# Two transformer layers with self- and cross-attention: rows of maxima and cross queries in four transfers each instead of eight

## The chip, the cores and the metric

The kernel runs on one core of a Trainium2 chip. The metric is the device time of one execution in microseconds, as the median of several runs. The core's engines are TensorE (PE in the profile, its weight loads PEld), VectorE (DVE), ScalarE (ACT), GpSimd (POOL) and SyncE (SP), which here only issues DMA transfers.

## The reference

Two layers work on x of shape (4, 512, 320) in float32. Each layer is self-attention, cross-attention to a context of 1601 positions and 192 channels, and a gated feed-forward block. There are 20 heads of 16 channels.

```
def _attn(x, ctx, wq, wk, wv, wo, bo, heads):     # dh = 16, scale = dh ** -0.5
    sim = einsum('bhid,bhjd->bhij', q, k) * scale
    a = softmax(sim, axis=-1)
    out = einsum('bhij,bhjd->bhid', a, v)
    return out @ wo + bo

h1 = _ln(x, n1_g, n1_b); x = _attn(h1, h1,      q1, k1, v1, o1_w, o1_b, 20) + x
h2 = _ln(x, n2_g, n2_b); x = _attn(h2, context, q2, k2, v2, o2_w, o2_b, 20) + x
h3 = _ln(x, n3_g, n3_b)
a, g = split(h3 @ ff_w1 + ff_b1, 2)
x = a * gelu(g) @ ff_w2 + ff_b2 + x
```

## The kernel before

**Units.** The attention of one batch is cut into five groups of four heads. One such group is a unit, and the kernel works through 20 self units, 20 cross units and 4 feed-forward units per layer, one after the other. A self unit has 512 keys in 4 chunks of 128, a cross unit 1601 keys in 13 chunks, the last of 65.

**Layout.** Each of a unit's four heads has a slot of 32 partitions, so that four products with 32 contraction rows can stand in four row strips of TensorE. Numbers are split in a high part (rounded to the fast float32 format) and a low part. In a slot of `kT` the even rows hold high parts of the keys and the odd rows low ones. Queries are copied to both, in `u.qbuf` of [128, 2, 512]: e = 0 holds the high part and e = 1 the low part, each as 512 columns. A score is then two passes, e = 0 and e = 1, which add up in PSUM.

**Maxima and scores.** For softmax the maximum of each query's scores is needed. Scores are therefore made twice: once with the queries on the partitions (`passes`, L1007), from which VectorE takes maxima (L1026), and once with the keys on the partitions (`product`, L1186), from which ScalarE makes the exponential (L1199). The maxima of the next unit are taken beside the scores of the present one; `round_of` issues scores of two heads and maxima of two others together. Two such rounds go by for each chunk, 8 in a self unit and 26 in a cross unit.

**`max_end` (L1067).** It turns a unit's negated maxima into rows. The high parts are 16 columns (4 heads by 4 query tiles), the low parts 16 more; VectorE transposes the [128, 32] tile in blocks of 32 (L1074), and DMA transfers then take rows of it to `u.mrow`: in the slot of head j the high part goes to row 32j and the low part to row 32j + 1. That is a transfer for each of four blocks and for each of the two parts, eight per unit, 2 KB each (L1080). `less_maximum` (L1189) is a third pass, which adds these two rows to every key's scores: `units_of`, all ones, is its stationary operand, `u.mrow[two_rows]` the moving one. The exponential waits for it. There are two `mrows`, used in turn.

**`queries` (L788).** It projects a unit's queries, ScalarE scales them into a stage tile (L802), `split` makes high and low parts on GpSimd (L695, L696), and transfers (L807) carry them to `u.qbuf`, for two halves i of the 512 columns and for even and odd rows s. A self unit's queries are made in one part, with four transfers of 128 KB. A cross unit's are made in two parts of 128 columns of each half, each with a stage tile and four transfers of 64 KB of its own.

**Order.** The order of all instructions is fixed when the program is built. Small steps stand in queues with due times; one of them, `slots`, holds the transfers that `slots_soon` puts there, of which up to four are given out per round, in order, from two rounds after they were put there. A new stage tile first gives out all older groups but one. A unit's maxima may begin three rounds after its last query and key transfer has been given out (`at_hand`). At the start, transfers are split over SyncE's and ScalarE's queues; from the first unit on all go through SyncE's queue, which takes them strictly in order: a transfer that waits for its data holds up all behind it.

Of the kernel before, what the change touches and what calls it, by code (L numbers as in the profile page):

```python
# [17 lines left out]
B, N, D = 4, 512, 320  # L18
# [108 lines left out]
def kernel(ctx: ExitStack, tc: tile.TileContext, x, context, ws, out):  # L127
# [50 lines left out]

    nmax = [const.tile([P, HG * NQ], F32, name=f"nmax{i}") for i in range(2)]
    kbuf = [const.tile([P, 4 * QT + P], F32, name=f"kT{i}") for i in range(4)]  # L180
    qbuf = [const.tile([P, 2, N], F32, name=f"q{i}") for i in range(4)]

    mrows = [const.tile([P, N], F32, name=f"m{i}") for i in range(2)]
    units_of = const.tile([P, P], F32, name="units")
    nc.gpsimd.memset(units_of, 1.0)
    fill = qbuf[3][:, 0, :]
    see(nc.vector.memset(fill, 1.0))


# [502 lines left out]
    def split(x, high):  # L692

        eng = nc.vector if start["on"] else nc.gpsimd
        eng.tensor_scalar(high.bitcast(F32R), x, 1.0, None, ALU.mult)  # L695
        eng.tensor_tensor(x, x, high, ALU.subtract)  # L696

    def rows_of(t, s):

        return t.rearrange("(r s) n -> s r n", s=2)[s]  # L700
# [10 lines left out]
    def stages(kind="stage"):  # L711
        empty(kind, 1)
        if kind == "kstage":
            kstage.reverse()
            return kstage[0]
        t = two.tile([P, 2, N // 2], F32, tag="stage", name="stage")
        return [t[:, e] for e in range(2)] + [t]

    def slots_soon(us, fs, name, kind="stage"):

        fs = list(fs)
        done = fs.pop()

        def last():
            done()
            for u in us:
                setattr(u, name, -9 if start["on"] else clock["round"])

        group = deque(fs + [last])
        groups[kind].append(group)  # L730
        for u in us:
            u.slots.append(group)
        if start["on"]:
            empty(kind, 0)
        for _ in tuple(group):
            add("slots", 0.0, lambda: group and group.popleft()(), clock["round"] + 3, yes, ready_at(clock["round"] + 2))
# [4 lines left out]
    def add_proj(u):  # L741
# [42 lines left out]
                add(chain, 0.0, hold, due - 4, yes, lambda: "h" in u.own)  # L784

        parts = 2 if u.cross else 1

        def queries(part):  # L788
            w = N // 2 // parts
            at = [i * (N // 2) + part * w for i in range(2)]  # L790
            ps = step_bank([P, 512], "qps")
            for k, _, n in DK:
                for i, to, gs in tiles:
                    see(nc.tensor.matmul(  # L794
                        ps[to, :w],
                        lhsT=wq[:n, k, gs],
                        rhs=first.hT[:n, k, at[i] : at[i] + w],
                        start=(k == 0),
                        stop=(k == 2),
                    ))  # L800
            high, low, both = stages()
            see(nc.scalar.mul(low[:, :w], ps[:, :w], DH**-0.5))  # L802
            split(low[:, :w], high[:, :w])

            def move(s, i):
                queue = (nc.sync, nc.scalar)[s] if start["on"] else nc.sync
                queue.dma_start(  # L807
                    out=u.qbuf.rearrange("(r s) e n -> s r e n", s=2)[s][:, :, at[i] : at[i] + w],
                    in_=both[i * GD : (i + 1) * GD, :, :w],
                )  # L810

            slots_soon(
                [u], [lambda s=s, i=i: move(s, i) for i in range(2) for s in range(2)],
                "qwhen" if part == parts - 1 else "qpart",
            )
            if part == parts - 1:
                u.q = u.qbuf
                first.made["q"] += 1

        def keys():  # L820

# [172 lines left out]
    def max_pairs(u):  # L994

        full = u.nkeys // 512
        rest = u.nkeys - full * 512
        ns = full + (1 if rest else 0)
        u.nm = nmax[u.n % 2]
        u.pm = two.tile([P, NQ, HG, ns], F32, tag="pm", name="pm") if ns > 1 else None  # L1000

        def passes(heads, outs, queries, keys):

            def one_pass(e):
                for j, out in zip(heads, outs):
                    rows = slice(j * SLOT, (j + 1) * SLOT)
                    see(nc.tensor.matmul(  # L1007
                        out,
                        lhsT=u.q[rows, e, queries].bitcast(F32R),
                        rhs=u.kT[rows, keys].bitcast(F32R),  # L1010
                        start=(e == 0),
                        stop=(e == 1),
                    ))

            return [lambda e=e: one_pass(e) for e in range(2)]

        def full_two(heads, t, s):
            pss = [bank("sps") for _ in heads]
            if ns == 1:
                to = u.nm.rearrange("p (j t) -> p j t", t=NQ)[:, :, t]  # L1020
            else:
                to = u.pm[:, t, :, s]

            def reduce():
                for j, ps in zip(heads, pss):
                    see(nc.vector.tensor_reduce(to[:, j : j + 1], ps, AX.X, ALU.max, negate=(ns == 1)))  # L1026

            keys = slice(u.k0 + s * 512, u.k0 + (s + 1) * 512)
            return passes(heads, pss, slice(t * P, (t + 1) * P), keys), reduce

        def rest_two(heads):

            w = rest + rest % 2
            pss = [bank("sps") for _ in heads]
            todo = [
                f
                for t in range(NQ)
                for f in passes(
                    heads, [ps[:, t * w : (t + 1) * w] for ps in pss], slice(t * P, (t + 1) * P),
                    slice(u.nkeys - w, u.nkeys),  # L1040
                )
            ]

            def reduce():
                for j, ps in zip(heads, pss):
                    see(nc.vector.tensor_reduce(
                        u.pm[:, :, j, full], ps[:, : NQ * w].rearrange("p (t w) -> p t w", w=w), AX.X, ALU.max
                    ))

            return todo, reduce  # L1050

        pairs = [
            deque([lambda heads=heads, t=t, s=s: full_two(heads, t, s)] for s in range(full) for t in range(NQ))
            for heads in ((2, 3), (0, 1))
        ]
        if rest:
            for q, heads in zip(pairs, ((2, 3), (0, 1))):
                q.append([lambda heads=heads: rest_two(heads)])
        return pairs
# [7 lines left out]
    def max_end(u):  # L1067

        both = two.tile([P, SLOT], F32, tag="nm2", name="nm2")
        turned = two.tile([P, SLOT], F32, tag="turned", name="turned")  # L1070
        n = HG * NQ
        see(nc.vector.tensor_scalar(both[:, :n].bitcast(F32R), u.nm, 1.0, None, ALU.mult))
        see(nc.vector.tensor_tensor(both[:, n:], u.nm, both[:, :n], ALU.subtract))
        see(nc.vector.transpose(turned, both))  # L1074
        to = u.mrow.rearrange("(j s) (t i r) -> i s j t r", s=SLOT, t=NQ, r=SLOT)
        for i in range(P // SLOT):
            for e in range(2):
                rows = slice(i * SLOT + e * n, i * SLOT + (e + 1) * n)
                queue = (nc.sync, nc.scalar)[e] if start["on"] else nc.sync
                queue.dma_start(out=to[i, e], in_=turned[rows, :])  # L1080

    def add_finish(u):

# [88 lines left out]
    def main(u, give, nxt):  # L1172
# [5 lines left out]
        def score(c, j):  # L1178
            r = min(P, u.nkeys - c * P)
            rows = slice(j * SLOT, (j + 1) * SLOT)  # L1180
            st = bank("st")
            keys = u.kT[rows, u.k0 + u.cols[c] : u.k0 + u.cols[c] + r].bitcast(F32R)
            two_rows = slice(j * SLOT, j * SLOT + 2)

            def product(e):
                see(nc.tensor.matmul(st[:r, :], lhsT=keys, rhs=u.q[rows, e, :].bitcast(F32R), start=(e == 0), stop=False))  # L1186

            def less_maximum():
                see(nc.tensor.matmul(  # L1189
                    st[:r, :],  # L1190
                    lhsT=units_of[two_rows, :r].bitcast(F32R),
                    rhs=u.mrow[two_rows, :].bitcast(F32R),
                    start=False,
                    stop=True,
                ))

            def exponential():
                p = place()
                see(nc.scalar.activation(p[:r], st[:r], AF.Exp))  # L1199
                pr[c, j] = p  # L1200

            return [lambda: product(0), lambda: product(1), less_maximum], exponential
# [357 lines left out]
```

## Time and profile before

| | |
|---|---|
| median of 3 runs | 3174.94 us (3174.68 to 3178.04) |
| profiled execution, its own time | 3173.88 us |
| its span, first to last instruction | 3172.1 us |
| mean granted TensorE clock | 0.971 of full speed |
| busy: TensorE, VectorE, ScalarE, GpSimd | 3005.0, 2193.3, 1965.0, 1269.2 us |

By stages, from the profile's windows (the first product of scores is at 41 us):

| stage | window, us | TensorE busy, us | VectorE busy, us | ScalarE busy, us |
|---|---|---|---|---|
| self, layer 0 | 41 to 427 | 353.49 | 301.43 | 239.51 |
| cross, layer 0 | 427 to 1337 | 860.13 | 725.39 | 701.17 |
| feed-forward, layer 0 | 1337 to 1634 | 295.91 | 81.03 | 43.70 |
| self, layer 1 | 1634 to 2014 | 348.86 | 291.43 | 239.09 |
| cross, layer 1 | 2014 to 2890 | 838.18 | 707.86 | 697.64 |
| feed-forward, layer 1 | 2890 to 3172 | 278.71 | 63.02 | 37.43 |

In the profile's lines, `L1080 SPq` is an issue on SyncE's queue by line 1080 of the kernel; the transfer itself takes place later. `[1.46 <-DMA m<-turned]` behind an instruction says that its engine stood idle for 1.46 us before it, until a transfer into a tile `m` from a tile `turned` had landed.

### The profile page before, as it was taken

To read this page: it belongs to the slowest core of one execution; us is meant where nothing else is said; L and a number is where in the kernel's file an instruction comes from. 1 tells how busy PE (TensorE), PEld (TensorE's weight loads), DVE (VectorE), ACT (ScalarE), POOL (GpSimd) and SP (SyncE) were. 2 spreads that over 40 slices of the span, in tenths; PEclk is the share of its full clock that TensorE was granted. 3 is DMA by queue.
4 is the path that set the end of the run, shared out by engine and by line. 5 is a ranking of instruction groups with operands and counts; after the bars stand their busy time and mean duration, and the time that the engine had idled before them with its cause. 6 is when DMAs were issued, how large, how long until landed. Compare 5 with 4: busy or idle time off the path is not lost.

```text
span 3172.1 us, 94150 instructions
## 1 busy us (share of the span) xinstructions
PE 3005.0 (95%) x37842; PEld 1627.3 (51%) x37842; DVE 2193.3 (69%) x4315; ACT 1965.0 (62%) x4029; POOL 1269.2 (40%) x1449
## 2 busy tenths in 40 slices
PE   8899999999999999999998999999999999999999
PEld 4445455554555455355544555555555555544555
DVE  7778788778778778622256877887888888784221
ACT  3666557777778678811126765587778778785110
POOL 3445334544544444311114453345455455442000
PEclk8999999999999899999999999999999999999999
DMA  4333222211211211300113332222122221112000
GB/s 100 91 71 80 50 43 51 59 38 40 58 37 40 58 33 30 85 2 6 26 25 82 72 64 53 44 54 40 33 47 41 41 48 32 39 23 67 9 11 15
DMA packets 256589, 145.41 MB, mean 46 GB/s; under 512 B 150036, under 2 KB 246680, under 8 KB 256152
## 3 DMA queue, kind: packets, MB, share of 16 engines
q1 hardware_dynamic: 254888, 138.33, 19.8%
q8 instruction: 298, 4.88, 0.6%
q10 hardware_dynamic: 1264, 1.06, 0.2%
q14 instruction: 139, 1.14, 0.1%
HBM read 33.04 MB, written 7.93 MB: 13 GB/s over the span
## 4 chain that ended last, share of the span: by engine, by line
PE 67%; DVE 16%; SPq 5%; DMA 4%; issue 3%; POOL 3%; ACT 2%; ACTq 0%; DVEq 0%; POOLq 0%
PE av L1213 16%; PE st L1186 10%; PE fps L1308 9%; PE sps L1007 9%; DVE pm L1026 8%; PE yps L1363 5%; DVE nmax L1026 3%; PE st L1189 3%; PE ops L1124 3%; PE vps L961 3%; SPq L1080 3%; PE qps L794 2%; PE fps L1321 2%; PE kps L869 2%; DMA kT<-w 1%
## 5 line engine op out<-in xcount | busy, mean ns | idle before, releaser
L1026 DVE TENSOR_REDUCE pm<-sps 128x1 f32<-128x512 f32 x1920 | 1189.6, 679 | 100.8 <-PE sps L1007 89.7
L1007 PE MATMUL sps<-kT,q 32*128 32x512 f32 (+1 forms) x6400 | 1065.4, 408 | 33.3 <-DMA kT<-stage 10.8
L1199 ACT ACTIVATE pr<-st 128x512 f32<-128x512 f32 (+1 forms) x1710 | 906.6, 602 | 252.5 <-PE st L1189 243.6
L1186 PE MATMUL st<-q,kT 32*128 32x512 f32 (+1 forms) x5440 | 947.2, 441 | 32.9 <-ACT w L878 26.3
L1230 POOL TENSOR_TENSOR o<-o,pr 128x512 f32<-128x512 f32 x359 | 461.5, 1286 | 729.3 <-ACT pr L1229 707.3
L1213 PE MATMUL av<-pr,vals 128*32 128x512 f32 (+1 forms) x3420 | 655.0, 627 | 37.1 <-DVE pm L1026 12.1
L1186 PEld LDWEIGHTS st<-q,kT 32*128 32x128 f32 (+1 forms) x5440 | 476.5, 183 | 396.5 <-ACT pr L1199 140.0
L1007 PEld LDWEIGHTS sps<-kT,q 32*128 32x128 f32 x6400 | 552.6, 188 | 136.7 <-DVE pm L1026 25.9
L1189 PE MATMUL st<-m,units 2*128 2x512 f32 (+1 forms) x2720 | 544.9, 401 | 35.1 <-DMA m<-turned 33.2
L1199 ACT ACTIVATE wself<-st 128x512 f32<-128x512 f32 (+1 forms) x867 | 463.6, 602 | 92.6 <-PE st L1189 90.8
L1026 DVE TENSOR_REDUCE nmax<-sps 128x1 f32<-128x512 f32 x640 | 396.3, 679 | 142.1 <-PE sps L1007 110.8
L1213 PE MATMUL av<-wself,vals 128*32 128x512 f32 (+1 forms) x1734 | 380.4, 623 | 12.9 <-DVE pm L1026 7.7
L1230 POOL TENSOR_TENSOR o<-o,wself 128x512 f32<-128x512 f32 x191 | 245.3, 1284 | 329.4 <-ACT wself L1229 326.4
L1189 PEld LDWEIGHTS st<-m,units 2*128 2x128 f32 (+1 forms) x2720 | 254.8, 184 | 71.0 <-issue 39.6
L1331 ACT ACTIVATE pr<-fps,b 128x512 f32<-128x512 f32 x80 | 54.8, 688 | 373.4 <-PE fps L1321 266.1
L1308 PE MATMUL fps<-hT,w 128*128 128x512 f32 x640 | 285.0, 597 | 0.0
L1229 ACT COPY pr<-av 128x512 f32<-128x512 f32 x359 | 218.2, 608 | 35.0 <-PE av L1213 34.0
L1213 PEld LDWEIGHTS av<-pr,vals 128*32 128x32 f32 (+1 forms) x3420 | 91.9, 109 | 208.3 <-DVE pm L1026 98.3
L1308 PEld LDWEIGHTS fps<-hT,w 128*128 128x128 f32 x640 | 118.5, 190 | 149.4 <-issue 147.2
L695 POOL TENSOR_SCALAR stage<-stage 128x256 fp32r<-128x256 f32 (+1 forms) x155 | 107.3, 692 | 184.0 <-ACT stage L802 90.8
L869 PEld LDWEIGHTS kps<-ctxT,w 32*128 32x128 f32 (+1 forms) x4992 | 119.6, 167 | 51.6 <-ACT pr L1199 20.9
L498 POOL TENSOR_SCALAR root<-root 128x4 f32<-128x4 f32 x23 | 5.2, 227 | 326.0 <-DVE root L492 325.5
(100 smaller groups left out, 3297.4 us busy)
## 6 DMA issues: line engine op xcount, KB each, us to landing
kT<-w SPq DMA_DIRECT2D x240, 104.0 KB
q<-stage SPq DMA_DIRECT2D x320, 64.0 KB
q<-stage SPq DMA_DIRECT2D x154, 128.0 KB
aT<-o SPq DMA_DIRECT2D x320, 32.0 KB
m<-turned SPq DMA_DIRECT2D x636, 2.0 KB
kT<-stage SPq DMA_DIRECT2D x156, 64.0 KB
kT<-w SPq DMA_DIRECT2D x80, 72.0 KB
w<-in_L_xattn_ff_w_dram SPq DMA_DIRECT2D x20, 256.0 KB
```

Source lines behind the costliest of these rows:

```text
L695: eng.tensor_scalar(high.bitcast(F32R), x, 1.0, None, ALU.mult)
L869: see(nc.tensor.matmul(ps[to : to + n, :PIECE], lhsT=wk_q[rows, k, u.g * GD : u.g * GD + n], rhs=first.kvT[rows, k, at : at + PIECE], star ...
L1007: see(nc.tensor.matmul(out, lhsT=u.q[rows, e, queries].bitcast(F32R), rhs=u.kT[rows, keys].bitcast(F32R), start=(e == 0), stop=(e == 1),))
L1026: see(nc.vector.tensor_reduce(to[:, j : j + 1], ps, AX.X, ALU.max, negate=(ns == 1)))
L1186: see(nc.tensor.matmul(st[:r, :], lhsT=keys, rhs=u.q[rows, e, :].bitcast(F32R), start=(e == 0), stop=False))
L1189: see(nc.tensor.matmul(st[:r, :], lhsT=units_of[two_rows, :r].bitcast(F32R), rhs=u.mrow[two_rows, :].bitcast(F32R), start=False, stop=True,))
L1199: see(nc.scalar.activation(p[:r], st[:r], AF.Exp))
L1213: see(nc.tensor.matmul(ps[j * SLOT : (j + 1) * SLOT, :], lhsT=columns_of[:r, head : head + SLOT], rhs=pr.pop((c, j))[:r, :], start=True, s ...
L1229: see(nc.scalar.copy(vo, ps))
L1230: nc.gpsimd.tensor_tensor(u.o, u.o, vo, ALU.add)
L1308: see(nc.tensor.matmul(ps, lhsT=w1[:, k, i * FF + c * P : i * FF + (c + 1) * P], rhs=u.hT[:, k, :], start=ahead and k == 0, stop=not ahead ...
L1363: see(nc.tensor.matmul(ps[:, :D], lhsT=hid[c][:, t * P : (t + 1) * P], rhs=w2[:, c, :], start=(c == 0), stop=(c == NHC - 1),))
```

## The change

A unit's maxima go to rows 32j (high) and 32j + 16 (low) of the slot instead of 32j and 32j + 1. The columns of the tile before the transposition are put in the order head, part, tile, so that the 32 rows of one transposed block go out in one transfer to eight rows that lie 16 apart: four transfers of 4 KB per unit. At the start they are two per queue. The other rows of `mrows` are set to zero once, at the start, and `less_maximum` contracts all 32 rows of the slot.

`u.qbuf` becomes [128, 2, 2, 256]: first the half i, then the part e. A half's high and low parts then lie side by side both in the stage tile and in `u.qbuf`. A cross unit's two parts of queries are put into one stage tile, and its four transfers of 128 KB are given out after the second part; each row of a transfer is one piece of 2 KB. `passes` and `product` read the queries from the new places; `product` reads its 512 columns as two pieces of 256.

```
-    qbuf = [const.tile([P, 2, N], F32, name=f"q{i}") for i in range(4)]
+    qbuf = [const.tile([P, 2, 2, N // 2], F32, name=f"q{i}") for i in range(4)]
     mrows = [const.tile([P, N], F32, name=f"m{i}") for i in range(2)]
+    for m in mrows:
+        nc.gpsimd.memset(m, 0.0)
...
         def queries(part):
...
-            high, low, both = stages()
-            see(nc.scalar.mul(low[:, :w], ps[:, :w], DH**-0.5))
-            split(low[:, :w], high[:, :w])
+            if part == 0:
+                made["q"] = stages()
+            high, low, both = made["q"]
+            cols = slice(part * w, (part + 1) * w)
+            see(nc.scalar.mul(low[:, cols], ps[:, :w], DH**-0.5))
+            split(low[:, cols], high[:, cols])
+            if part < parts - 1:
+                return
             def move(s, i):
                 queue = (nc.sync, nc.scalar)[s] if start["on"] else nc.sync
                 queue.dma_start(
-                    out=u.qbuf.rearrange("(r s) e n -> s r e n", s=2)[s][:, :, at[i] : at[i] + w],
-                    in_=both[i * GD : (i + 1) * GD, :, :w],
+                    out=rows_of(u.qbuf[:, i].rearrange("p e n -> p (e n)"), s),
+                    in_=both[i * GD : (i + 1) * GD].rearrange("p e n -> p (e n)"),
                 )
...
-                        lhsT=u.q[rows, e, queries].bitcast(F32R),
+                        lhsT=u.q[rows, t // 2, e, t % 2 * P : (t % 2 + 1) * P].bitcast(F32R),
...
     def max_end(u):
-        n = HG * NQ
-        see(nc.vector.tensor_scalar(both[:, :n].bitcast(F32R), u.nm, 1.0, None, ALU.mult))
-        see(nc.vector.tensor_tensor(both[:, n:], u.nm, both[:, :n], ALU.subtract))
+        high, low = (both.rearrange("p (j e t) -> p e j t", j=HG, e=2)[:, e] for e in range(2))
+        nm = u.nm.rearrange("p (j t) -> p j t", t=NQ)
+        see(nc.vector.tensor_scalar(high.bitcast(F32R), nm, 1.0, None, ALU.mult))
+        see(nc.vector.tensor_tensor(low, nm, high, ALU.subtract))
         see(nc.vector.transpose(turned, both))
-        to = u.mrow.rearrange("(j s) (t i r) -> i s j t r", s=SLOT, t=NQ, r=SLOT)
+        to = u.mrow.rearrange("(n s) (t i r) -> s i n t r", s=DH, t=NQ, r=SLOT)[0]
         for i in range(P // SLOT):
-            for e in range(2):
-                rows = slice(i * SLOT + e * n, i * SLOT + (e + 1) * n)
-                queue = (nc.sync, nc.scalar)[e] if start["on"] else nc.sync
-                queue.dma_start(out=to[i, e], in_=turned[rows, :])
+            queue = (nc.sync, nc.scalar)[i % 2] if start["on"] else nc.sync
+            queue.dma_start(out=to[i], in_=turned[i * SLOT : (i + 1) * SLOT, :])
...
-                see(nc.tensor.matmul(st[:r, :], lhsT=keys, rhs=u.q[rows, e, :].bitcast(F32R), start=(e == 0), stop=False))
+                see(nc.tensor.matmul(st[:r, :], lhsT=keys, rhs=u.q[rows, :, e].bitcast(F32R), start=(e == 0), stop=False))
             def less_maximum():
-                    lhsT=units_of[two_rows, :r].bitcast(F32R),
-                    rhs=u.mrow[two_rows, :].bitcast(F32R),
+                    lhsT=units_of[rows, :r].bitcast(F32R),
+                    rhs=u.mrow[rows, :].bitcast(F32R),
```

More of the change, by code (lines that the diff above doesn't have):

```diff
@@ L180 @@
     kbuf = [const.tile([P, 4 * QT + P], F32, name=f"kT{i}") for i in range(4)]
-    qbuf = [const.tile([P, 2, N], F32, name=f"q{i}") for i in range(4)]
+    qbuf = [const.tile([P, 2, 2, N // 2], F32, name=f"q{i}") for i in range(4)]
     mrows = [const.tile([P, N], F32, name=f"m{i}") for i in range(2)]
+    for m in mrows:
+        nc.gpsimd.memset(m, 0.0)
     units_of = const.tile([P, P], F32, name="units")
     nc.gpsimd.memset(units_of, 1.0)
-    fill = qbuf[3][:, 0, :]
+    fill = qbuf[3][:, 0].rearrange("p e n -> p (e n)")
     see(nc.vector.memset(fill, 1.0))
@@ L786, in add_proj @@
         parts = 2 if u.cross else 1
+        made = {}
         def queries(part):
@@ L807, in move @@
                 queue.dma_start(
-                    out=u.qbuf.rearrange("(r s) e n -> s r e n", s=2)[s][:, :, at[i] : at[i] + w],
-                    in_=both[i * GD : (i + 1) * GD, :, :w],
-                )
[L812 to L818, printed above, removed]
+                    out=rows_of(u.qbuf[:, i].rearrange("p e n -> p (e n)"), s),
+                    in_=both[i * GD : (i + 1) * GD].rearrange("p e n -> p (e n)"),
+                )
+            slots_soon([u], [lambda s=s, i=i: move(s, i) for i in range(2) for s in range(2)], "qwhen")
+            u.q = u.qbuf
+            first.made["q"] += 1
         def keys():
@@ L1000, in max_pairs, with passes @@
         u.pm = two.tile([P, NQ, HG, ns], F32, tag="pm", name="pm") if ns > 1 else None
-        def passes(heads, outs, queries, keys):
+        def passes(heads, outs, t, keys):
             def one_pass(e):
@@ L1028, in full_two @@
             keys = slice(u.k0 + s * 512, u.k0 + (s + 1) * 512)
-            return passes(heads, pss, slice(t * P, (t + 1) * P), keys), reduce
+            return passes(heads, pss, t, keys), reduce
         def rest_two(heads):
@@ L1038, in rest_two @@
                 for f in passes(
-                    heads, [ps[:, t * w : (t + 1) * w] for ps in pss], slice(t * P, (t + 1) * P),
-                    slice(u.nkeys - w, u.nkeys),
+                    heads, [ps[:, t * w : (t + 1) * w] for ps in pss], t, slice(u.nkeys - w, u.nkeys),
                 )
@@ L1182, in score @@
             keys = u.kT[rows, u.k0 + u.cols[c] : u.k0 + u.cols[c] + r].bitcast(F32R)
-            two_rows = slice(j * SLOT, j * SLOT + 2)
             def product(e):
-                see(nc.tensor.matmul(st[:r, :], lhsT=keys, rhs=u.q[rows, e, :].bitcast(F32R), start=(e == 0), stop=False))
+                see(nc.tensor.matmul(st[:r, :], lhsT=keys, rhs=u.q[rows, :, e].bitcast(F32R), start=(e == 0), stop=False))
             def less_maximum():
```

## The prediction

> **What bounds the kernel now.** I read the profile's page first (busy shares and the chain that ended last), then the list of waits, then the timeline round single waits, at last the lines by form for prices. The page:
>
> ```profile
> span 3172.1 us, 94150 instructions
> PE 3005.0 (95%) x37842; PEld 1627.3 (51%) x37842; DVE 2193.3 (69%) x4315; ACT 1965.0 (62%) x4029; POOL 1269.2 (40%) x1449
> PE 67%; DVE 16%; SPq 5%; DMA 4%; issue 3%; POOL 3%; ACT 2%; ACTq 0%; DVEq 0%; POOLq 0%
> ```
>
> TensorE is the bound: busy for 95% of the span, so all the time that any change can win without removing matmuls lies in its 167 us of idle time. The chain's 9% on SyncE's queue and on transfers says that part of that idle time comes from moving data. The list of waits says which part (microseconds in total, times, longest):
>
> ```profile
> PE st L1189 <- DMA m<-turned: 33.2, 25, 6.9
> PE st L1186 <- ACT w L878: 26.3, 15, 2.6
> PE av L1213 <- DVE pm L1026: 19.8, 26, 1.4
> PE av L1213 <- DVE nmax L1026: 13.5, 28, 1.0
> PE sps L1007 <- DMA kT<-stage: 10.8, 5, 2.8
> ```
>
> The largest single wait of TensorE is the one that the change touches: the subtracting product (L1189) waits for the row of maxima, 33.2 us in 25 places. What such a wait consists of shows the timeline of one, in a self unit:
>
> ```profile
> 1904.52 3.35 SPq L1080 DMA_DIRECT2D m<-turned  x6
> 1907.97 2.45 SPq L839 DMA_DIRECT2D kT<-stage  x4
> 1909.12 0.50 PE L1189 MATMUL st<-m,units 2*128 2x512 f32 x2 [1.46 <-DMA m<-turned]
> 1909.68 2.06 ACT L1199 ACTIVATE pr<-st 128x512 f32<-128x512 f32 x4 [1.82 <-PE st L1189]
> 1910.08 1.29 DVE L1026 TENSOR_REDUCE nmax<-sps 128x1 f32<-128x512 f32 x2 [1.22 <-PE st L1189]
> ```
>
> The transfers leave SyncE's queue one after the other; the last is issued by 1907.87 and the product starts 1.25 us later, so the landing is short and the issuing is the long part. In this wait TensorE (1.46), ScalarE (1.82) and VectorE (1.22) all sat idle: no other work was waiting to take its place.
>
> **The change part by part.** *Maxima in four transfers.* One batch of eight, and what an issue costs by its kind:
>
> ```profile
> 105.16 4.64 SPq L1080 DMA_DIRECT2D m<-turned  x8
> ...
> 116.90 2.45 SPq L839 DMA_DIRECT2D kT<-stage  x4
> ...
> L1080 SPq DMA_DIRECT2D m<-turned x636: 520/521/1123, 36.2 to 2860.5; - x159
> L807 SPq DMA_DIRECT2D q<-stage x474: 590/607/1931, 17.6 to 2814.2; - x158
> ```
>
> Eight take 4.64 us, 0.58 each with the step between. An issue of 16 rows (m) takes 521 ns, one of 64 rows (q) 607 ns, so 32 rows should lie between, near the first: four take 2.3 us, and the last maximum is under way 2.3 us earlier. If each doubled in price nothing would be won, if it stayed exactly at 521 ns 2.32; I take 2.3. The landing could grow, as each transfer now holds 4 KB; the 1.25 us above are mostly latency, so I take no change (0.3 more would cost 25 x 0.3 = 7.5 us at most).
>
> Capping each of the 25 waits at 2.3 us leaves only the longest above the cap: 33.2 - (6.9 - 2.3) = 28.6 us.
>
> A cross unit shows the same with a queue in front:
>
> ```profile
> 845.69 2.54 SPq L807 DMA_DIRECT2D q<-stage  x4
> 846.79 0.21 DVE L1074 STREAM_TRANSPOSE turned<-nm 128x32 f32<-128x32 f32 x1
> 848.35 4.62 SPq L1080 DMA_DIRECT2D m<-turned  x8
> 850.05 3.81 DVE L1026 TENSOR_REDUCE pm<-sps 128x1 f32<-128x512 f32 x6 [0.69 <-PE sps L1007]
> 854.12 0.50 PE L1189 MATMUL st<-m,units 2*128 2x512 f32 x2 [1.50 <-DMA m<-turned]
> ```
>
> The maxima were ready at 847.0 but left from 848.35, behind four transfers of half the queries. Here VectorE worked until 853.86, only 0.26 us before the product: what TensorE wins here, it partly meets again as a bank that VectorE has not read.
>
> *What else hangs on the queue.* The eight issues at 105.16 stand ahead of keys in an unbroken row of issues, and TensorE waits for both a query stage and a key:
>
> ```profile
> 104.89 1.51 PE L826 MATMUL kps<-hT,wself 112*32 112x256 f32 x12 [4.87 <-ACT stage L802]
> 120.91 0.49 PE L1007 MATMUL sps<-kT,q 32*128 32x512 f32 x2 [1.68 <-DMA kT<-stage]
> L802 ACT ACTIVATE stage<-qps 128x256 f32<-128x256 f32 x40 | 15.4, 385 | 51.4 <-PE qps L794 36.7 <-DMA q<-stage 7.1 <-DMA aT<-o 2.1
> ```
>
> Of the 10.8 us on keys about 9.8 go when capped at 2.3 each (none is over 2.8), and of the 4.87 us, behind a query transfer (7.1 on ScalarE's side), 2.3.
>
> *The start.* There both queues issue four; now two each:
>
> ```profile
> 36.48 3.24 ACTq L1080 DMA_DIRECT2D m<-turned  x4
> 4.96 0.21 POOL L185 MEMSET units<- 128x128 f32 x1
> 13.72 3.54 POOL L570 TENSOR_TENSOR x<-x,brow 128x320 f32<-128x320 f32 x4 [8.56 <-DMA brow<-in_L_xattn_o_b_dram]
> ```
>
> Two of 0.6 us go: 1.2 us. The two added memsets of 512 columns stand beside the 128-column one of 0.21 us: at most 0.84 us each by columns, inside GpSimd's 8.56 us of idle time before 13.72. Without that cover they would cost 1.7 us.
>
> *Cross queries.* 40 units issue four fewer each: 160 x 0.61 = 98 us less on SyncE's queue, but TensorE meets it only where queries stand ahead of maxima, and there the cap of 2.3 already exceeds the wait of 1.50. What it adds: the first half's transfers now wait for GpSimd's split of the second half, and whatever is queued behind them on SyncE (maxima, keys, attention outputs) waits too. They were needed together before, too (a unit's maxima begin three rounds after the last query transfer is given out), so I price it at nothing; if a round's delay of 1.7 us (876 us of the second cross stage below over 20 units of 26 rounds) hit all 40 units it would cost 68 us. The 26.3 us on L878 stay: they wait for transfers of context keys, whose issue waits for GpSimd's split of them, not for maxima.
>
> *Products.* The subtracting product contracts 32 rows instead of 2, and the main product reads its queries as two pieces of 256:
>
> ```profile
> L1189 PE MATMUL st<-m,units x2720: 384/394/791, 41.1 to 2890.1; 2*128 2x512 f32 x183, 2*65 2x512 f32 x12
> L1186 PE MATMUL st<-q,kT x5440: 382/397/791, 37.4 to 2889.8; 32*128 32x512 f32 x183, 32*65 32x512 f32 x12
> L878 ACT COPY w<-kps 128x104 f32<-128x104 f32 x160 | 31.6, 249 | 100.1 <-PE kps L869 53.9 <-DMA kT<-w 42.2 <-issue 2.2
> L834 ACT COPY stage<-kps 128x256 f32<-128x256 f32 x40 | 14.9, 373 | 48.1 <-PE kps L826 44.4 <-DMA m<-turned 3.2 <-DMA q<-stage 0.6
> L969 ACT COPY vals<-vps 128x192 f32<-128x192 f32 x48 | 13.0, 323 | 32.5 <-PE vps L961 32.5
> ```
>
> Medians of 394 ns for 2 rows and 397 for 32: 3 ns x 2720, two at a time, is 4 us at the very worst and nothing by the minima (384 and 382). For the split read no matmul of this trace is a pattern. The nearest row is ScalarE's: two whole copies (249 ns at 104 columns, 373 at 256) give 0.82 ns a column and 321 ns at 192; the copy that writes its 192 columns in 12 pieces takes 323. A piece costs it nothing, so I take nothing here. The upper end is a second start of a matmul:
>
> ```profile
> L794 PE MATMUL qps<-hT,w 112*32 112x128 f32 x1280 | 51.6, 280 | 0.4 <-DVE pm L1026 0.4
> L794 PE MATMUL qps<-hT,wself 112*32 112x256 f32 x640 | 48.4, 425 | 0.0
> ```
>
> Half the columns save 145 ns, so 135 ns do not depend on them: 5440 passes, two at a time, 2720 x 0.135 = 367 us if it showed in full. Fewer than 512 columns are not streamed, so it can't be a gain.
>
> *The sum.* 28.6 + 9.8 + 2.3 + 1.2 = 42 us of idle time can go. How much comes back: in the self unit 1.22 of 1.46 us were idle on all three engines, in the cross unit only 0.26 of 1.50 on VectorE. Between these (84% and 17%), weighted to the self stages, to which all of the key terms and the longest waits belong, I keep 70%: 29 us. The profiled execution took 3173.88 us, its span and 1.8 us around it; it comes to 3144.9. The median of the three runs lies 1.06 higher, so I predict 3146 us.
>
> [...]
>
> **The rivals.** *The waits are handed on.* After each stall VectorE's reduces (the waits on L1026 above, 19.8 + 13.5 us) or the next transfer end last; kept is the cross unit's share, 17 to 20%: 8 us, 3167. For it: the 3.81 us of reduces before 854. Against: the idle ScalarE and VectorE at 1909.
>
> *Slower by the order.* Fewer query transfers shift the order that the queue of small steps is drained in, so from the first cross stage on the instructions stand in another order than before; the self stages keep theirs. The cross stages hold this much idle time:
>
> ```profile
> 427.00:1337.00 910.00, 860.13 (x12406) 471.36 (x12404) 725.39 (x1397) 701.17 (x1454) 434.76 (x441) 0.97 0.21 47
> 2014.00:2890.00 876.00, 838.18 (x12396) 462.51 (x12393) 707.86 (x1355) 697.64 (x1451) 434.90 (x441) 0.98 0.20 45
> ```
>
> 50 + 38 = 88 us. If worse placed context keys and maxima add half of it, 44, the sum is 15 us slower: 3190. It decides from a third (29 us) on. For it: the waits on L878 and L1026 stand there and hang on such placing. Against: work and rounds are the same, and the queue has less to carry.
>
> *Slower by the split read.* 10 ns for each of 2720 pairs of passes eats the gain; 20 ns give 54 - 29 = 25 us more: 3200.
>
> *It doesn't shorten the wait.* If an issue of 32 rows costs twice one of 16, or landing grows by 2 us, only the start is left: 3173. Against: 607 ns for 64 rows.
>
> **How the numbers follow.** Forecast 0.67 (3146, its own range 3133 to 3163), handed on 0.15, order 0.08, split read 0.06, no shorter wait 0.04. A difference of 0.2% is 6.3 us, about what a measurement of this kernel can tell from none: faster below 3168.6, slower above 3181.3. Faster: 0.67 and half of the second, 0.75; the same: the other half and the last, 0.11; slower 0.14. Range 3125 (all 42 us kept, and 8 won by the order) to 3176 (the last case, and 3 lost by the order): it takes in all but the slower cases.
>
> **What would show it.** Right: four issues of m in 2.3 us; the wait of L1189 for m under 10 us, that of L1007 for keys under 3; span of the self stages down by some 10 us each, that of the cross stages by 4 or 5 each; L1186 still at a median of 397. Wrong: m's issues over 0.8 us each; L1186 longer; idle time before L1213 and L1186 up by as much as m's fell; cross stages longer than 910 and 876 us.

## The result, and the profile after

| | before | after |
|---|---|---|
| median, timed side by side (4 runs each) | 3176.32 us (3174.68 to 3178.04) | 3101.56 us (3099.82 to 3104.63) |
| profiled execution, its own time | 3173.88 us | 3100.62 us |
| mean granted TensorE clock | 0.971 | 0.986 |

The ratio is 0.9766 (95% interval 0.9749 to 0.9783): 75 us faster, where 29 were forecast. The time lies below the predicted range. The changed kernel's page, the first lines and the chain:

```profile
span 3098.8 us, 93413 instructions
PE 2966.7 (96%) x37842; PEld 1615.6 (52%) x37842; DVE 2192.6 (71%) x4315; ACT 1963.5 (63%) x4029; POOL 1269.3 (41%) x1451
PE 70%; DVE 20%; DMA 2%; issue 2%; POOL 2%; ACT 2%; SPq 1%; ACTq 0%; POOLq 0%; DVEq 0%
```

SyncE's queue and transfers fell from 9% of the chain to 3%. The span is 73.3 us shorter, and only half of that is idle time of TensorE: 167.1 us before (3172.1 - 3005.0), 132.1 now (3098.8 - 2966.7), so 35.0. The other 38.3 us are TensorE's *busy* time, 3005.0 to 2966.7, with the same 37842 matmuls. The matmuls themselves became faster.

The list of TensorE's waits (total, times, longest):

```profile
PE st L1187 <- ACT w L882: 27.3, 15, 2.9
PE av L1214 <- DVE pm L1030: 20.5, 28, 1.3
PE av L1214 <- DVE nmax L1030: 11.6, 27, 1.3
PE sps L1011 <- DMA kT<-stage: 4.8, 3, 2.4
PE st L1190 <- DMA m<-turned: 2.8, 2, 2.3
PE kps L830 <- ACT stage L808: 2.4, 1, 2.4
```

The wait for maxima is all but gone (33.2 us in 25 places before), that for keys more than halved (10.8). The two waits on VectorE in this list did not take their place: 32.1 us now, 33.3 before. All of TensorE's waits on VectorE's maxima together, small ones on other lines included, rose from 39.8 to 44.8 us, so some 5 us were handed on. Lines by form:

```profile
L1082 SPq DMA_DIRECT2D m<-turned x318: 587/638/1463, 36.3 to 2786.5; - x159
L1190 PE MATMUL st<-m,units x2720: 382/392/627, 40.3 to 2816.9; 32*128 32x512 f32 x183, 32*65 32x512 f32 x12
L1187 PE MATMUL st<-q,kT x5440: 382/397/792, 37.7 to 2816.6; 32*128 32x512 f32 x183, 32*65 32x512 f32 x12
```

An issue of 32 rows takes 638 ns where one of 16 took 521, and four take 2.63 us together:

```profile
101.62 2.63 SPq L1082 DMA_DIRECT2D m<-turned  x4
```

The subtracting product (392 ns) and the split read (397) cost what they did. The longest product is 792 ns, twice the median: matmuls at half clock. The windows by stage, in the order of the table of before, without the feed-forward ones; the last three columns are the granted clock, the DMA share and GB/s:

```profile
40.30:405.70 365.40, 346.81 (x5146) 188.90 (x5148) 302.56 (x619) 239.17 (x495) 168.14 (x213) 0.96 0.34 75
405.70:1292.10 886.40, 841.37 (x12397) 463.16 (x12394) 719.94 (x1395) 700.17 (x1453) 434.79 (x441) 0.99 0.21 48
1587.90:1948.80 360.90, 342.21 (x5197) 187.06 (x5190) 295.39 (x594) 239.26 (x496) 165.19 (x199) 0.98 0.30 66
1948.80:2817.20 868.40, 833.09 (x12391) 462.39 (x12385) 709.17 (x1353) 697.79 (x1450) 434.40 (x441) 0.99 0.20 45
```

The first cross stage shows it best: 23.6 us shorter (910.0 to 886.4), of which 4.8 are idle time (49.9 to 45.0) and 18.8 busy time, with the clock at 0.99 instead of 0.97. The self stages lost 20.6 and 19.1 us, the second cross stage 7.6.

**What the clock does.** In the records (74 entries before, 40 after) it stands at 1.0 or 0.5 and nothing between. Summed over the trace's clock record it was at 0.5 for 187.5 us in 37 stretches before, and for 85.8 us in 20 stretches after (a second trace of the changed kernel, from `e9_after_again` below, has 116.4 us in 23). Had TensorE been busy in all of them, 101.7 us less at half clock would save half of that, 51 us, by estimate; 38.3 were measured. Here is one stretch, in the kernel before, in the second cross stage; first the timeline, then windows of 3.4 us:

```profile
2195.03 4.61 SPq L1080 DMA_DIRECT2D m<-turned  x8
2200.96 0.50 PE L1189 MATMUL st<-m,units 2*128 2x512 f32 x2 [1.69 <-DMA m<-turned]
```

```profile
2194.37:2197.79 3.42, 3.42 (x40) 1.41 (x44) 3.39 (x6) 3.30 (x8) 1.63 (x2) 1.00 0.30 56
2197.79:2201.20 3.41, 1.72 (x40) 1.11 (x36) 2.04 (x4) 1.20 (x4) 2.16 (x3) 1.00 0.04 8
2201.20:2204.60 3.40, 3.40 (x28) 1.04 (x28) 1.29 (x2) 2.52 (x5) 0.06 (x1) 0.55 0.31 59
2204.60:2208.00 3.40, 3.40 (x28) 1.15 (x20) 2.77 (x5) 2.20 (x5) 1.28 (x1) 0.50 0.10 18
2208.00:2211.40 3.40, 3.17 (x44) 1.56 (x44) 2.98 (x6) 2.64 (x6) 0.00 (x0) 0.95 0.00 0
```

The eight issues end at 2199.6, the product stands idle for 1.69 us, and TensorE is busy for only 1.72 us of that window. In the next two windows it is busy throughout, at half clock, and does 28 matmuls in each where it did 40: the price of the stall is paid a second time after it has ended. (By the clock's record the stretch lasts from 2201.54 to 2208.37; the windows shown begin 0.34 us earlier, hence the 0.55 and the 0.95.) In the list of waits there is no trace of this part.

### The profile page after: what moved, and what is told of

Same layout as the page of the kernel before. It is cut to its first block, busy times and chain, and to the rows that moved or that the text cites. A ratio compares the mean times of both kernels' runs of the same rounds, so it can differ in the third digit from the quotient of the medians.

```text
span 3098.8 us, 93413 instructions
## 1 busy us (share of the span) xinstructions
PE 2966.7 (96%) x37842; PEld 1615.6 (52%) x37842; DVE 2192.6 (71%) x4315; ACT 1963.5 (63%) x4029; POOL 1269.3 (41%) x1451
## 3 DMA queue, kind: packets, MB, share of 16 engines
q8 instruction: 297, 4.87, 0.7%
## 4 chain that ended last, share of the span: by engine, by line
PE 70%; DVE 20%; DMA 2%; issue 2%; POOL 2%; ACT 2%; SPq 1%; ACTq 0%; POOLq 0%; DVEq 0%
PE av L1214 17%; PE st L1187 10%; DVE pm L1030 9%; PE fps L1309 9%; PE sps L1011 9%; PE yps L1364 6%; DVE nmax L1030 5%; PE ops L1126 3%; PE qps L797 3%; PE vps L965 3%; PE st L1190 3%; PE fps L1322 2%; PE kps L873 2%; PE vps L947 1%; DMA kT<-w 1%
## 5 line engine op out<-in xcount | busy, mean ns | idle before, releaser
L1187 PE MATMUL st<-q,kT 32*128 32x512 f32 (+1 forms) x5440 | 943.8, 437 | 36.8 <-ACT w L882 27.3
L1187 PEld LDWEIGHTS st<-q,kT 32*128 32x128 f32 (+1 forms) x5440 | 480.5, 181 | 395.6 <-ACT pr L1200 136.3
L1214 PE MATMUL av<-pr,vals 128*32 128x512 f32 (+1 forms) x3420 | 642.9, 614 | 37.6 <-DVE pm L1030 12.4
L1011 PEld LDWEIGHTS sps<-kT,q 32*128 32x128 f32 x6400 | 546.4, 185 | 137.2 <-DVE pm L1030 30.4
L1190 PE MATMUL st<-m,units 32*128 32x512 f32 (+1 forms) x2720 | 534.1, 393 | 2.8 <-DMA m<-turned 2.8
L1214 PE MATMUL av<-wself,vals 128*32 128x512 f32 (+1 forms) x1734 | 373.1, 612 | 12.9 <-DVE pm L1030 8.1
L1190 PEld LDWEIGHTS st<-m,units 32*128 32x128 f32 (+1 forms) x2720 | 251.4, 182 | 21.9 <-issue 2.7
```

What stands on the lines that cost most here:

```text
L1011: see(nc.tensor.matmul(out, lhsT=u.q[rows, t // 2, e, t % 2 * P : (t % 2 + 1) * P].bitcast(F32R), rhs=u.kT[rows, keys].bitcast(F32R), star ...
L1187: see(nc.tensor.matmul(st[:r, :], lhsT=keys, rhs=u.q[rows, :, e].bitcast(F32R), start=(e == 0), stop=False))
L1190: see(nc.tensor.matmul(st[:r, :], lhsT=units_of[rows, :r].bitcast(F32R), rhs=u.mrow[rows, :].bitcast(F32R), start=False, stop=True,))
L1214: see(nc.tensor.matmul(ps[j * SLOT : (j + 1) * SLOT, :], lhsT=columns_of[:r, head : head + SLOT], rhs=pr.pop((c, j))[:r, :], start=True, s ...
```

## The experiments

The theories that the expectations name by letters, in short: **A**, fewer issues end TensorE's stalls, and each stall avoided also saves the half-clock stretch that would have followed it; **B**, the queries' part (98 us less on SyncE's queue) is worth a good part of the gain; **C**, contracting 32 rows instead of 2 keeps the clock up by itself; **D**, the clock falls for some reason other than the stalls, so that filling them changes nothing; **E**, the number of issues decides, and not the order in which the heads' rows leave. Times are medians; each ratio is to the kernel before on the same chip (3178.65 us for the first four kernels, 3179.20 for the next four, 3174.74 for the last four).

**The maxima's part alone**: `max_end`, `less_maximum` and the memsets as in the change, queries as before.

> The kernel before with only the maxima's part of the change: four transfers of a unit's maxima, 32 rows contracted; queries as before. Theory A (shorter waits, and the clock with them): the maxima's shorter issue takes away the waits for m and for keys behind them, and each wait taken away also takes away a stretch at half clock, so most of the 75 us are here: 45 to 60 us faster, half-clock time of TensorE down from 188 us to 100 to 120. Rival B (the queries do it): 20 to 30 us, what the idle time alone is worth, and half-clock time near 188. Rival C (the 32-row product is quicker by itself): the same as A here, told apart by e3.

3098.21 us, ratio 0.9745 (0.9723 to 0.9767), clock 0.986. The whole gain is here, and more than A expected; a second time it gave 0.9766 (below).

**The queries' part alone**: `qbuf`, `queries`, `passes` and `product` as in the change, maxima as before.

> The kernel before with only the queries' part: new layout of the query buffer, one stage tile and four transfers for a cross unit; maxima as before in eight transfers, two rows contracted. Theory A: 10 to 25 us faster, all of it in the cross stages, the wait of L1189's product for m still near 25 to 30 us. Rival B: 40 to 50 us faster. Rival C: 10 to 25.

3177.19 us, ratio 0.9991 (0.9979 to 1.0003), clock 0.970:

```profile
PE st L1191 <- DMA m<-turned: 24.5, 22, 5.9
PE 3010.3 (95%) x37842; PEld 1630.2 (51%) x37842; DVE 2194.1 (69%) x4315; ACT 1965.7 (62%) x4029; POOL 1267.4 (40%) x1449
```

The wait for maxima fell by 8.7 us, and nothing came of it. B falls, and so does A's own price for this part. It also shows that a stall has no fixed price: in this trace TensorE's idle time is 6.4 us shorter than before, but its busy time 5.3 us longer, with 194.0 us at half clock.

**32 rows alone**: the kernel before, its eight transfers kept, with only this edit:

```
+    for m in mrows:
+        nc.gpsimd.memset(m, 0.0)
...
-                    lhsT=units_of[two_rows, :r].bitcast(F32R),
-                    rhs=u.mrow[two_rows, :].bitcast(F32R),
+                    lhsT=units_of[rows, :r].bitcast(F32R),
+                    rhs=u.mrow[rows, :].bitcast(F32R),
```

> The kernel before with only the subtracting product contracting 32 rows (the rows that no transfer writes are zero); transfers as before. Theory A and rival B: within 4 us of the kernel before, half-clock time near 188 us. Rival C (more active rows keep the clock up, or the product is quicker): 20 to 40 us faster with the waits for m unchanged at 33 us.

3163.85 us (10 runs, 3154.91 to 3176.45), ratio 0.9953 (0.9937 to 0.9969): 15 us faster, with 32 rows contracted instead of 2 and no transfer changed. The profiled execution happened to be the slowest of the ten, so its lines bound the effect from one side only:

```profile
core 0: 3174.7 us, clock 0.970
PE st L1190 <- DMA m<-turned: 31.6, 26, 4.6
PE sps L1009 <- DMA kT<-stage: 12.7, 7, 2.8
```

The waits are those of before. What differs is the clock: 0.970 to 0.978 over the ten runs, 0.975 in the mean, where the 19 runs of the kernel before beside it had 0.965 to 0.970, 0.968 in the mean. C holds in part: the effect is there, at less than the 20 to 40 us expected, and no trace of a faster run shows how it comes about.

**Eight transfers in the changed kernel**: each of the four cut in two, heads 0 and 1 apart from 2 and 3.

```
-            queue = (nc.sync, nc.scalar)[i % 2] if start["on"] else nc.sync
-            queue.dma_start(out=to[i], in_=turned[i * SLOT : (i + 1) * SLOT, :])
+            for h in range(2):
+                queue = (nc.sync, nc.scalar)[h] if start["on"] else nc.sync
+                rows = slice(i * SLOT + h * DH, i * SLOT + (h + 1) * DH)
+                queue.dma_start(out=to[i][h * HG : (h + 1) * HG], in_=turned[rows, :])
```

> The changed kernel with each of its four transfers of maxima cut in two again (eight of 2 KB, same rows as in the changed kernel), all else as changed. Theory A: the waits for m come back to 20 to 33 us, half-clock time to 130 to 180 us, 35 to 55 us slower than the changed kernel (3137 to 3157). Rival B: 10 to 20 us slower than the changed kernel. Rival C: no slower than 15 us.

3151.74 us, ratio 0.9908 (0.9891 to 0.9925), clock 0.978:

```profile
PE sps L1011 <- DMA kT<-stage: 15.1, 8, 4.0
PE st L1192 <- DMA m<-turned: 11.9, 11, 3.2
```

By the ratios the number of transfers alone is worth 45 us ((0.9908 - 0.9766) x 3176), as A expected. Both waits come back, that for maxima to 11.9 us instead of the 20 to 33 expected, and half-clock time rises from 85.8 to 143.0 us (116.4 in the second trace of the changed kernel).

**The stalls filled in the kernel before.** In the 23 units where the subtracting product waited, TensorE is given passes ahead of it whose moving operand is zero: 228 matmuls more, added into the same banks. `fills` gives the number of passes for each of these units, `none` is a tile of zeros, and `opened` holds the banks of heads 0 and 1. No transfer is touched.

```
+    none = const.tile([P, 8], F32, name="none")
+    nc.gpsimd.memset(none, 0.0)
...
+            if c == 0 and j < 2:
+                opened[j] = st
...
+                for _ in range(fills.get(u.n, 0) if c == 0 and j == 0 else 0):
+                    for h in range(2):
+                        at = slice(h * SLOT, (h + 1) * SLOT)
+                        nc.tensor.matmul(
+                            opened[h], lhsT=u.kT[at, u.k0 : u.k0 + P].bitcast(F32R),
+                            rhs=none[at].rearrange("p (o n) -> p o n", o=1).to_broadcast([SLOT, N // 8, 8]).bitcast(F32R),
+                            start=False, stop=False,
+                        )
```

> The kernel before, unchanged in its transfers, with idle products put into the waits for m: ahead of a unit's first subtracting product, in the 23 units that waited over 0.3 us in the profile of before, as many passes as fit into that wait (0.235 us each, two heads at a time, moving operand all zero, so the scores stay as they are). The row of maxima lands when it did. Theory A (a stall also costs a stretch at half clock): TensorE is busy in the wait and the stretches that followed those waits (48 of 188 us at half clock) get fewer: 10 to 24 us faster with not a transfer changed. Rival D (the clock falls for another reason, few active rows for one, and the stalls only cost their idle time): 0 to 5 us slower.

3169.21 us (9 runs), ratio 0.9968 (0.9956 to 0.9979):

```profile
core 0: 3169.9 us, clock 0.975
PE st L1204 <- DMA m<-turned: 11.8, 20, 1.8
PE sps L1011 <- DMA kT<-stage: 11.8, 6, 2.8
PE 3019.3 (95%) x38070; PEld 1644.2 (52%) x38070; DVE 2193.9 (69%) x4315; ACT 1964.0 (62%) x4029; POOL 1269.4 (40%) x1450
```

10 us faster for doing more: the product can't start before its rows have landed, so this gain is not the stall's own time. The clock was 0.973 to 0.977 over the nine runs, 0.964 to 0.970 over the 13 of the kernel before beside them. Half-clock time is 163.0 us against 187.5. Each stretch can be put down to the wait that takes most of the idle time in the window ahead of it: nine stretches of the kernel before, 47.8 us, stand behind waits for maxima; here two are left, 13.7 us. D falls; A holds, at the low end of its range; 11.8 us of the waits were left unfilled, and with other causes there are still 31 stretches in all.

**17 rows in the changed kernel**, from the row of the high part to that of the low part.

```
+            some = slice(j * SLOT, j * SLOT + DH + 1)
...
-                    lhsT=units_of[rows, :r].bitcast(F32R),
-                    rhs=u.mrow[rows, :].bitcast(F32R),
+                    lhsT=units_of[some, :r].bitcast(F32R),
+                    rhs=u.mrow[some, :].bitcast(F32R),
```

> The changed kernel with its subtracting product contracting rows 0 to 16 of the slot instead of 0 to 31 (both rows of maxima are among them). [...] If the rows do not matter: within 4 us of the changed kernel (3098 to 3106).

3107.15 us, ratio 0.9778 (0.9764 to 0.9792). That is 1 us above the range expected if the rows do not matter. The difference from the changed kernel is 4 us by the ratios, but the intervals overlap, so it was run again beside the changed kernel itself:

> The changed kernel itself, as the measure for the three others, timed on the same chip with them: ratio to the kernel before 0.976 (0.974 to 0.979), about 3102 us, clock 0.98 to 0.99.

3103.96 us, ratio 0.9771 (0.9748 to 0.9794).

> The changed kernel with a subtracting product that contracts 17 rows of the slot (from the high part's row to the low part's) instead of 32, for a second time, now beside the changed kernel. If the number of rows moves the granted clock, 17 rows stand between 2 and 32: 32 rows alone were worth 15 us, so 17 should cost 4 to 8 us against the changed kernel (ratio 0.978 to 0.9795) with a clock lower by 0.001 to 0.003. If rows don't matter, the ratios of the two kernels agree within 0.0005 (1.5 us).

3110.85 us, ratio 0.9793 (0.9771 to 0.9816), clocks 0.978 to 0.983 where the changed kernel's were 0.981 to 0.987. Slower both times, by 4 and 7 us, and both times within what these runs can't tell from none: likely, not shown.

**Eight transfers, the first two heads' rows ahead.** As above, with the two loops exchanged: `for h in range(2): for i in range(P // SLOT):`, so that four issues carry all that the first pair of products needs.

> The changed kernel with eight transfers of maxima as in e4, but those of heads 0 and 1 first: a unit's first product needs only the first four. Theory A (what counts is when the first product's rows have landed): waits for m fall from 12 us to under 5 us, and the time to 3100 to 3125, what is left being keys behind the longer batch. Rival E (it is the number of issues on the queue, whatever their order): as e4, 3146 to 3155.

3148.55 us, ratio 0.9901 (0.9884 to 0.9917):

```profile
PE sps L1011 <- DMA kT<-stage: 14.9, 8, 4.0
PE st L1192 <- DMA m<-turned: 13.6, 13, 3.7
```

The order wins nothing of what A expected; E was right. In 9 of the 13 places it is now the pair of heads 2 and 3 that waits, 1.2 us after the last of eight issues, and the keys behind the batch come as late as before.

**Context keys further apart.** The largest wait left, L1187 on ACT's copy of context keys, hangs on how often pieces of them are handed out: every four rounds in the changed kernel, here every six. The same number also sets when the first piece, and the context tile ahead of it, are due: six rounds earlier here.

```
-            ... else (due - 10, 4)
+            ... else (due - 10, 6)
```

> The changed kernel with the pieces of a cross unit's context keys due 6 rounds apart instead of 4, meant to take away the largest waits that are left (27 us for the stage tile on L882, with half-clock stretches behind most of them). Theory A: if the waits fall by half, 14 us of idle time and some 10 to 15 us of half-clock loss go: 3075 to 3090. If the due times do not decide where the pieces come to stand: within 6 us of the changed kernel; if the pieces come to collide with others, up to 20 us slower.

3164.43 us, ratio 0.9954 (0.9941 to 0.9968): 60 us slower than the changed kernel by the ratios, against the expectation.

```profile
core 0: 3163.9 us, clock 0.976
PE st L1187 <- ACT w L882: 54.0, 16, 4.9
PE 3003.3 (95%) x37842; PEld 1636.5 (52%) x37842; DVE 2194.4 (69%) x4315; ACT 1965.0 (62%) x4029; POOL 1272.3 (40%) x1451
```

The wait doubled, by 26.7 us; TensorE's busy time grew by 36.6 at the same matmuls. A stall of another kind costs the clock in the same way: 14 half-clock stretches, 109.2 us, stand behind these waits, where the two traces of the changed kernel have 4 (13.7 us) and 7 (34.1 us). The expectation had put a stretch behind most of the changed kernel's waits; it was 4 stretches for 15 waits. Whether the distance of the pieces or the earlier start lengthened the waits is not separated. The opposite step, three rounds apart and the first piece due three rounds later, was tried on the maxima's part alone, beside a second run of that:

> The part of the change that concerns the maxima, for a second time, with the kernel's queries as before. If the queries' part is worth nothing it agrees with the changed kernel within 0.0010 (3 us). If its shorter wait (no query part held back until the second half is split) is worth something, it is 3 to 6 us faster than the changed kernel, as its first run hinted (3098.2 against 3101.6 us).

3103.02 us, ratio 0.9766 (0.9747 to 0.9786): the changed kernel's time. The queries' part neither adds nor takes.

```
-            ... else (due - 10, 4)
+            ... else (due - 10, 3)
```

> The maxima's part alone, and the pieces of a cross unit's context keys handed out every three rounds instead of every four. Six rounds apart instead of four made the changed kernel 63 us slower and doubled the waits for these keys (27.3 to 54.0 us). If the waits move evenly with this distance, three apart lowers them to some 15 us, and the time by 10 to 20 us, to about 3085. The rival: pieces closer together meet TensorE's own work with the queue more often, other transfers come later, and the time stays within 5 us of the maxima's part alone or goes above it.

3088.71 us, ratio 0.9721 (0.9700 to 0.9742): 14 us faster than the maxima's part with four rounds, and faster than the changed kernel; the intervals of kernels on this chip don't meet. (That of the first run of the maxima's part, 0.9723 to 0.9767, does reach into it.) It is the fastest version found.

```profile
core 0: 3089.8 us, clock 0.985
PE st L1186 <- ACT w L880: 18.4, 13, 1.9
```

The run beside it, with four rounds:

```profile
PE st L1186 <- ACT w L880: 22.2, 14, 2.4
```

The wait fell less than expected, the time as expected. Between these two traces TensorE's idle time differs by 1.2 us only (124.9 to 123.7) and its busy time by 10.5, so the gain lies in the clock (0.985 in this trace, 0.981 in the other) and not in shorter waits; what brought it is not shown.

## Why the prediction was wrong, point by point

**The sum** is the step that failed: it priced a stall of TensorE at its idle time and nothing else. Its premise was that all the time that a change can win without removing matmuls lies in TensorE's 167 us of idle time. As idle time it was nearly right. The terms were 28.6, 9.8, 2.3 and 1.2 us, 42 in all, of which 70% were to be kept; the rows show 30.4 (33.2 to 2.8), 6.0 (10.8 to 4.8), 2.5 (4.87 to 2.4) and 0.8 (the first subtracting product stands at 40.3 us, not 41.1), 39.7 in all, and idle time fell by 35.0, as some 5 us were handed on to waits on VectorE: 83% of the forecast's 42, where 70% were expected. What had no term is the 38.3 us of busy time. The page that the prediction read first showed a clock of 0.971, and the table of times repeats it; at 1.0 or 0.5 that means 184 us at half clock (2 x 0.029 x 3172.1), but the sum makes no use of it, as if the stalls had no part in it. That they cause it is shown by the filled stalls (10 us won with no transfer touched), and again by the doubled waits for context keys. Nine of the 37 half-clock stretches of before begin in or right behind the window in which the subtracting product had waited, 47.8 us together, and four more, 13.7 us, behind waits for keys; in the trace of after none and one are left. So 16 of the 25 waits brought no stretch, and these two kinds account for 58 of the 101.7 us by which half-clock time fell. Another 27 us (41.0 to 13.7; 34.1 in the second trace of after) went from behind the waits for context keys, though these did not get shorter (26.3 us, now 27.3). Why, and where the rest comes from, stays open.

**The issue's price** was mis-sized: 0.58 us with the step, it measured 0.66 (2.63 us for four). Four instead of eight save 2.0 us, not 2.3; that still covers all but 3 of the 25 waits (2.2, 2.3 and 6.9 us).

**32 rows at nothing** was right for the product's duration (392 ns, 394 before) and wrong for the time: alone they win 15 us, through the clock. With the 45 us of four instead of eight transfers this makes 60 of the 75 us; the rest is not separated. Part of it is the layout's own: with eight transfers in the changed kernel the waits are 11.9 us, not 33.2. There the first pair of products needs only the first seven and starts 0.5 to 0.8 us after the last issue, where it was 1.1 us or more; and the queries' part alone had lowered the waits to 24.5. That two edits each keep the clock up need not add evenly either.

**Right**: the split read costs nothing (397 ns both); the cross queries are worth nothing beside the four transfers of maxima (that they are worth nothing without these too, though the waits fell by 8.7 us, the reasoning did not give); the waits on ACT's copies stay (26.3 us, now 27.3); only 5 us are handed on to VectorE. Right also that the issuing, not the landing, makes the wait: with the same bytes in eight transfers 45 us are lost. The landing did not grow with 4 KB instead of 2 KB: in the longer of the two waits that the trace of after has left, the product at 1677.75 us starts 1.22 us after the last of the four issues, where it was 1.25 us at 1909.12 in the trace of before. Even keys of 64 KB take not much longer there: the product at 120.91 us starts 1.56 us after the last of their issues.

**The stages** were forecast as 10 us for each self stage and 4 or 5 for each cross stage; they gave 20.6, 19.1, 23.6 and 7.6. The first three are some twice the forecast or more. In the two self stages 13.9 and 12.5 us of it are idle time and 6.7 each busy time; in the first cross stage 4.8 and 18.8. The forecast had no busy time in any of them. One price for each microsecond of stall doesn't give these numbers either: in the first cross stage something more kept the clock up, and whether it was the 32 rows, or where the waits fell in the windows, is not separated.

## What to carry to other kernels

Where TensorE is the bound, read the granted clock as part of the bill for each stall. On this kernel 35.0 us less idle time came with 38.3 us less busy time in one trace, and 38.9 with 25.2 in the second trace of the changed kernel; with the later context keys 26.7 us of waits brought 36.6. The list of waits shows only the first half of this bill. It is an average and no price for a single stall: many waits brought no half-clock time, and the queries' part removed 8.7 us of waits for nothing. Look at windows of 3.4 us ahead of and behind a stall to see what it costs. Count the issues between the last producer and the waiting product, and prefer few larger transfers there (here four of 4 KB instead of eight of 2 KB were worth 45 us). Where a stall can't be removed, harmless passes in it can be worth more than they cost (228 of them won 10 us here).

## What the runs showed of the hardware

**Short stalls suffice.** In the clock's record of the trace of before all 74 entries begin on one grid of 3413.33 ns, within 5 ns.

In the stretch shown above, 1.69 us of idle time in one window brought two windows at half clock. Over the whole trace of before, laid on this grid, 20 of the 21 full-clock windows with 1.5 us or more of idle time were followed by a window at half clock, 7 of the 27 with 1.0 to 1.5 us, and 9 of the 825 with less. (In the trace of after it is 9 of 14, 3 of 26 and 7 of 841, so 1.5 us is no sharp bound.) The length of a wait alone did not decide: in the trace of after, waits for context keys of 2.84 and 2.87 us lay across an edge of the grid, with 1.3 us on one side and 1.5 on the other, and brought no half clock.

**Idle time does not sort all windows.** TensorE was busy for all of 3.40 us in the window from 2201.2 on and stayed at half clock for another. The windows of the trace of before can be sorted by the idle time of the window ahead of each, to tell the 54 at half clock from the others. At the value that sorts them best, 1.53 us, it mis-sorts 30 of 927. What else moves the clock is not shown: contracting 32 rows instead of 2 brought 15 us, at a mean clock of 0.975 instead of 0.968, and no trace here tells how.

**The scatter between runs is the clock too.** Four runs of the changed kernel on one chip had spans of 3108.1, 3106.0, 3098.3 and 3096.1 us at clocks of 0.981, 0.982, 0.986 and 0.987: some 2 us for each 0.001. One look at this kernel can be 10 us off.
